# A fused attention and mixture-of-experts block on one core: the transposes of the next four tiles' rows are put at the end of the attention unit

## The chip, the cores and the metric

The kernel runs on one core of a Trainium2 chip. That core has five engines that each work through their own list of instructions in order: PE (TensorE, matrix products; the profile shows its weight loads as a row of their own, PEld), DVE (VectorE), ACT (ScalarE), POOL (GpSimd) and SP (SyncE, which here only issues DMAs). They meet through semaphores. The metric is the device time of one execution in microseconds (us), lower is better.

## The reference

The block is one layer: gated attention, then a mixture of experts, each on a layer norm of x and each added to x.

```
h  = layernorm(x)                                  # x: 32 batches x 128 tokens x 128
q, k, v    = h @ Wqkv + bqkv                       # 16 heads of 8
qa, ka, va = ctx_1024 @ Wqkv_aux + bqkv_aux
o  = softmax(q k' / sqrt 8) v * (1 - sigmoid(g)) + softmax(q ka' / sqrt 8) va * sigmoid(g)
x  = x + tanh(g_xattn) * (o @ Wo + bo)
h  = layernorm(x)
s  = sigmoid(h @ gate_w.T)                         # 64 experts in 8 groups of 8
# by s + gate_bias: the best 4 groups (sum of the two best), in them the best 8 experts
w  = 2.5 * s[chosen] / sum(s[chosen])
y  = sum over the chosen e of w_e * (silu(h @ Wg_e) * (h @ Wu_e)) @ Wd_e
y += (silu(h @ Ws_gate) * (h @ Ws_up)) @ Ws_down
x  = x + tanh(g_ffn) * y
```

All of it is float32.

## The kernel before, in words

**Two kinds of work on one list.** The 32 batches are attended in 64 units, one batch and one kind of keys (own or context) each, in the loop `for u in range(NU + 5)` near the end of the kernel. The experts' work is woven into these units, since attention alone leaves engines free. For the first seven of the eight blocks of four batches, each token's row is scattered to a table in DRAM (`xslot`), in tiles of 128 rows that belong to one expert group; there are two such tables, of 14 times four tiles and 18 times four tiles. The eighth block is computed with all experts at the end.

**A unit.** In the order of the code: `queries(u-1)` transposes the negated row maxima `nm` into PSUM (`nt`, line 580) and DVE adds them to the queries (`qa`, line 582). `scores_max(u)` makes the scores (`sp`, line 554) and DVE reduces them to `nm` (line 563, two instructions). `turn` may start a job of the experts. Then, in alternation, a step of the last batch's output (`ot`, `at`, `mt`, `msb`, `yp`: lines 639 to 667) or of the next batch's projections (`tp`, `pp`, `vp`: lines 293 to 360). `values(u-2)` is `op` (line 623), `softmax(u-1)` is the second scores `st` (line 600, it reads `qa`) and the exponentials on ACT (line 610). `add_up` finishes an earlier job: `y` (line 1054) and the next transposes `ht` (line 1041). Steps of the routing (`route`, lines 700 to 900) and scatters (line 869 on POOL, with a small memset at line 868 ahead of each) are dealt out over the unit; `use_bank` is the last place for a step that needs PSUM.

**A job** is one tile: `group_hidden` multiplies it with the gate and the up weights of its expert group (`gu`, line 1026), ACT takes the tanh (line 949), DVE multiplies twice (lines 950 and 954), POOL applies the routing weights `wq` (line 958). Two jobs later `group_turn` and `group_down` follow. Once attention is over, `alone` is true.

**Beginning four tiles.** Tiles are fetched four at a time. `load_rows_of` issues the DMA of 512 rows from the table into the only buffer `xq` (SP, line 985). `begin_tiles` reads four table entries into PE registers (line 997), transposes the four tiles on PE (line 1004), lets POOL multiply the routing columns with a mask (`wg`, line 1006), DVE reduce them to `wq` (line 1013) and ACT copy the transposes out of PSUM (`xqT`, line 1015). `pair` calls it for the next four tiles when the first job of four has just been issued.

**What sets the order.** The engines' lists are written in the order of the calls (a manual schedule), so a call that moves in the code moves its instructions on PE, POOL, DVE, ACT and SP. **PSUM:** `banks` hands out three buffers of two banks in turn, to `sp` (two), `gu`, `st` (two), `ht`, the transposes of `begin_tiles` and most routing steps; each waits for the reader of the tile that was given the same buffer three requests before. `bank` hands out two single banks in turn, to `nt`, `op`, `mt`, `ot`, `vp`, `pp`, `y` and others.

Of the kernel before, what the change touches and what calls it, by code (L numbers as in the profile page):

```python
# [51 lines left out]
def gated_block_kernel(  # L52
# [44 lines left out]
    def banks(name):  # L97
        return ps_s.tile([P, 2, 512], F32, tag="s", name=name)
# [578 lines left out]
    def scatter_some(n):  # L677

        for _ in range(min(n, len(to_scatter))):
            f, *a = to_scatter.pop(0)  # L680
            f(*a)
# [279 lines left out]
    def hidden(t, n):  # L961


        m = P if n < NPAIR else F
        if n < NPAIR and n % 2 == 0 and n:
            load_weights(t, n // 2 + 5)
        gu = banks(f"gu{t}_{n}")
        for i, (wr, ws) in enumerate(((wg_sb, wsg_sb), (wu_sb, wsu_sb))):
            lhsT = wr[:, 2 * n : 2 * n + 2, :].rearrange("p e f -> p (e f)") if n < NPAIR else ws
            nc.tensor.matmul(gu[0:m, i], lhsT, xT[t], start=True, stop=True)  # L970
        gate = cws.pop((t, n)) if n < NPAIR else None
        if t < S1:
            h = rt.tile([P, TB], F32, tag="wT", name=f"hs{t}")
        else:
            h = hp.tile([P, TB], F32, tag="h", name=f"h{t}_{n}", bufs=LAG + 1)
        return silu_times(f"{t}_{n}", m, gu, gate, alone, h)
# [4 lines left out]
    def load_rows_of(c, q):  # L981
        if q >= NQ[c]:
            return
        xq = rt.tile([P, QS, NW], F32, tag="xq", name=f"xq{c}_{q}")
        k = nc.sync.dma_start(
            out=xq,
            in_=xslot[c][q * QS * P : (q + 1) * QS * P].rearrange("(a p) d -> p a d", p=P),
        ).ins
        for name in scatters[c]:
            tc.add_manual_dep(k, name, AFTER)  # L990
        rows_of[c, q] = xq

    def begin_tiles(c, q):

        xq = rows_of.pop((c, q))
        v = [
            nc.tensor.value_load(
                table[c][0:1, q * QS + a : q * QS + a + 1], min_val=0, max_val=NG - 1
            )
            for a in range(QS)  # L1000
        ]
        tp = banks(f"xq{c}_{q}t")
        for a in range(QS):
            nc.tensor.transpose(tp[:, 0, ts(a, P)], xq[:, a, 0:D], ident)
        every = rt.tile([P, QS, EG, NG], F32, tag="wg", name=f"wg{c}_{q}")
        nc.gpsimd.tensor_tensor(  # L1006
            every,
            xq[:, :, D:NW].rearrange("p a (g e) -> p a e g", e=EG),
            mine[c][:, ts(q, QS), :].unsqueeze(2).to_broadcast([P, QS, EG, NG]),
            ALU.mult,  # L1010
        )
        wq = rt.tile([P, QS, EG], F32, tag="wq", name=f"wq{c}_{q}", bufs=2)
        V.tensor_reduce(wq, every, AX.X, ALU.add)
        xt = rt.tile([P, QS * P], F32, tag="xqT", name=f"xqT{c}_{q}", bufs=2)
        nc.scalar.copy(xt, tp[:, 0])
        parts_of[c, q] = [xt, wq, v, None]

    def group_hidden(c, q, n):

        if n == 0:  # L1020
            parts_of[c, q][3] = alone
        xt, wq, v, later = parts_of[c, q]
        gu = banks(f"gu{c}_{q}_{n}")
        for i, w in enumerate((wg_sb, wu_sb)):
            w = w.rearrange("p (g e) f -> p g (e f)", g=NG)
            nc.tensor.matmul(  # L1026
                gu[:, i],
                xt[:, ts(n, P)],
                w[:, ds(v[n], 1), :].rearrange("p o f -> p (o f)"),
                start=True,  # L1030
                stop=True,
            )
        h = hp.tile([P, TB], F32, tag="h", name=f"h{c}_{q}_{n}", bufs=LAG + 1)
        gate = wq[:, n, :].unsqueeze(2).to_broadcast([P, EG, F])
        return silu_times(f"{c}_{q}_{n}", P, gu, gate, later, h)
# [118 lines left out]
    def finish(t, ysb, w):  # L1154

        yt = bank(f"yt{t}")
        for k in range(BG // w):
            for i in range(k * w, (k + 1) * w):
                nc.tensor.transpose(yt[:, ts(i, P)], ysb[:, ts(i, P)], ident)
            xs = x_sb[t][:, ts(k, w), :]  # L1160
            V.tensor_tensor(
                xs.rearrange("p t d -> p (t d)"),
                yt[:, ts(k, w * P)],
                xs.rearrange("p t d -> p (t d)"),
                ALU.add,
            )
            b0 = t * BG + k * w
            nc.sync.dma_start(out=out[b0 : b0 + w].rearrange("b t d -> t b d"), in_=xs)
# [9 lines left out]
    alone = False  # L1178
# [22 lines left out]
    def ready(job):  # L1201
        if job[0] == "all":
            return job[1] < routed
        return job[1] in started and clock - started[job[1]] >= (2 if alone else 3)

    def pair():

        nonlocal fresh
        if todo and ready(todo[0]):
            kind, *job = todo.pop(0)  # L1210
            fresh = True
            if kind == "all":
                waiting.append((job, hidden(*job)))
            else:
                waiting.append((job, group_hidden(*job)))
                c, q, n = job
                if n == 0 and q + 1 < NQ[c]:
                    begin_tiles(c, q + 1)
                    load_rows_of(c, q + 2)


    turned = []
# [25 lines left out]
    def route_some(n, free=False):  # L1248

        nonlocal routed, takes_bank  # L1250
        for _ in range(n):
            if not routing or takes_bank and not free:
                return
            free = False
            takes_bank = next(routing[0], None)
            if takes_bank is None:
                routing.pop(0)
                routed += 1

    def use_bank():  # L1260
        if ended:
            finish(*ended.pop(0))
        else:
            route_some(1, True)
# [11 lines left out]
    def more(it):  # L1276
        next(it, None)
# [27 lines left out]
    def turn(there):  # L1305

        if there:
            pair()
        round_begins()
        scatter_some(1)  # L1310
        gather_some(1)

    for u in range(NU + 5):
        if 10 <= u:
            for k in islice(clear, 1):
                tc.add_manual_dep(k.ins, reached[min(u, NU) - 1], AFTER)
        if 1 <= u <= len(weight_loads):
            for k in weight_loads[u - 1]():
                tc.add_manual_dep(k.ins, reached[u - 1], AFTER)
        if 0 <= u - 1 < NU:  # L1320
            queries(u - 1)
        if u == 0:
            first, steps = steps, prepare(1)
            more(steps)
            more(steps)
        if u < NU:
            scores_max(u)
        if u == 0:
            finish_gates()
            more(first)  # L1330
            ictx.close()
            rt = ctx.enter_context(tc.tile_pool(name="rt", bufs=1))
            hp = ctx.enter_context(tc.tile_pool(name="hp", bufs=2))
            clear_values(1)
            count_tables()
            nc.gpsimd.memset(lower, 1.0)
            nc.gpsimd.affine_select(
                out=lower,
                in_=lower,
                compare_op=ALU.is_gt,  # L1340
                fill=0.0,
                base=0,
                pattern=[[1, NG], [-1, NG]],
                channel_multiplier=0,
            )
        k = u % UA
        n = plan(u)

        turn(n > 0)
        if k % 2 == 0:  # L1350
            more(outputs)
        else:
            more(steps)
        osb = values(u - 2) if 0 <= u - 2 < NU else None
        if osb is not None:
            finished = output((u - 2) // 2, osb)
        if 0 <= u - 1 < NU:
            softmax(u - 1)
        add_up()
        copy_some()  # L1360
        if osb is not None:
            outputs = finished
        route_some(1)
        turn(n > 1)
        more(outputs)
        copy_some()
        route_some(2)
        add_up()
        turn(n > 2)
        if u:  # L1370
            more(steps)
        route_some(1)
        add_up()
        if k == 2 and u < NU - UA - 2:
            coming = prepare((u + 2) // UA + 1)
            more(coming)
        elif k == 3:
            more(coming)
            steps, coming = coming, iter(())
        use_bank()  # L1380
        turn(False)
        copy_some()
    share_banks()
    alone = True
# [65 lines left out]
```

## Time and profile before

| | |
|---|---|
| median of 12 runs | 1046.75 us (1043.0 to 1049.41) |
| the profiled execution | 1049.55 us, its span 1047.8 us |
| mean clock granted to PE | 0.962 of full speed |
| PE busy | 942.3 us, 90% |
| DVE, POOL, ACT busy | 607.3, 540.6, 494.8 us |
| first call of `begin_tiles` (transposes) | 330.1 us |
| end of attention's weave (first `h<-th,wq` on DVE) | 602.4 us |
| transposes of `begin_tiles` in between, seven calls | 340.9, 384.0, 423.8, 469.0, 509.0, 542.9, 573.1 us |

A time "at 423.8" is counted from the start of the span. Rows of the timeline give start, duration, engine, line, what is written from what, and in brackets how long the engine had been idle before and what released it. An engine idle beside a busy PE costs nothing; PE idle during attention adds to the span unless something later gives it back.

### The profile page before, as it was taken

How to read it: one execution, taken by the hardware profiler on the slowest of the kernel's cores; microseconds unless marked ns; L12 is line 12 of the kernel's file. 1: busy time of each engine (PE TensorE's matmuls, PEld its weight loads, DVE VectorE, ACT ScalarE, POOL GpSimd, SP SyncE). 2: the span in 40 equal slices, each digit the busy share in tenths (PEclk: the TensorE clock that was granted, in tenths of full speed). 3: DMA queues.
4: the chain of work that ended last, by engine and by line, in shares of the span. 5: the costliest groups of instructions: out<-in, count | busy, mean ns of one | idle time of the engine just before them, and what ended most of it. 6: DMA issues, size and time to landing. Idle time of an engine off the chain costs nothing.

```text
span 1047.8 us, 20766 instructions
## 1 busy us (share of the span) xinstructions
PE 942.3 (90%) x7704; PEld 637.2 (61%) x7704; DVE 607.3 (58%) x1248; ACT 494.8 (47%) x943; POOL 540.6 (52%) x867
## 2 busy tenths in 40 slices
PE   6999889788897989989999799998999999999876
PEld 5777566566674666656666466665666666764332
DVE  5566776657763665575666374553455555546453
ACT  2566456454554455455544344644555555542111
POOL 3435368588576265855763767511333342007770
PEclk8899999889998999999999899999999999999989
DMA  5544234101011000100110122244222222115530
GB/s 142 129 117 151 96 116 161 44 25 48 7 39 58 22 17 24 61 19 28 39 60 16 55 81 74 78 107 113 77 84 77 76 76 69 41 51 141 142 85 25
DMA packets 100008, 75.19 MB, mean 72 GB/s; under 512 B 23943, under 2 KB 92167, under 8 KB 99911
## 3 DMA queue, kind: packets, MB, share of 16 engines
q1 hardware_dynamic: 90662, 55.11, 18.6%
q0 software_dynamic: 8960, 18.36, 5.6%
q8 instruction: 65, 1.06, 0.4%
q10 hardware_dynamic: 288, 0.39, 0.1%
q14 instruction: 33, 0.26, 0.1%
HBM read 39.63 MB, written 34.21 MB: 70 GB/s over the span
## 4 chain that ended last, share of the span: by engine, by line
PE 56%; POOL 18%; DVE 13%; issue 5%; DMA 4%; ACT 3%; SPq 1%; POOLq 0%; ACTq 0%; DVEq 0%
PE gu L1026 17%; PE y L1054 9%; PE st L600 5%; POOL yg L1095 5%; POOL xslot L869 4%; PE op L623 4%; PE ht L1041 4%; PE sp L554 4%; DVE nm L563 3%; PE pp L305 2%; PE gu L970 2%; POOL bd L268 2%; PE nt L580 2%; POOL row L234 1%; DMA yg<-yslot,place 1%
## 5 line engine op out<-in xcount | busy, mean ns | idle before, releaser
L954 DVE TENSOR_TENSOR th<-gu,th 128x512 f32<-128x512 f32 x158 | 109.0, 690 | 159.2 <-ACT th L947 157.4
L947 ACT ACTIVATE th<-gu 128x512 f32<-128x512 f32 (+1 forms) x132 | 78.9, 597 | 195.8 <-PE gu L1026 107.0
L563 DVE TENSOR_REDUCE nm<-sp 128x8 f32<-128x1024 f32 x128 | 150.7, 1218 | 18.1 <-PE sp L554 17.9
L1054 PEld LDWEIGHTS y<-wd_sb,hT 128*128 128x128 f32 x1008 | 129.7, 193 | 47.3 <-issue 45.7
L610 ACT ACTIVATE pt<-st 128x1024 f32<-128x1024 f32 x128 | 124.1, 1021 | 49.8 <-PE st L600 49.8
L1026 PE MATMUL gu<-wg_sb,xqT 128*128 x252 | 134.3, 615 | 3.1 <-DVE th L954 2.5
L1054 PE MATMUL y<-wd_sb,hT 128*128 x1008 | 136.3, 279 | 0.9 <-ACT hT L1043 0.9
L1095 POOL DMA_INDIRECT yg<-yslot,place x112 | 111.5, 995 | 43.4 <-issue 30.9
L1026 PE MATMUL gu<-wu_sb,xqT 128*128 x252 | 129.7, 596 | 0.0
L869 POOL DMA_INDIRECT xslot<-row,place x112 | 114.2, 1020 | 21.9 <-issue 20.9
L268 POOL TENSOR_SCALAR bd<-qk,mask 128x256 f32<-128x256 f32 x90 | 83.2, 934 | 45.2 <-ACT qk L321 44.5
L1006 POOL TENSOR_TENSOR wg<-xq,mine 128x256 f32<-128x256 f32 x32 | 24.6, 770 | 135.5 <-DMA xq<-xslot 121.8
L623 PE MATMUL op<-pt,v 128*32 128x128 f32 x2048 | 71.6, 282 | 25.4 <-DVE qa L582 24.8
L1026 PEld LDWEIGHTS gu<-wu_sb,xqT 128*128 128x128 f32 x252 | 48.6, 193 | 61.6 <-issue 61.6
L554 PE MATMUL sp<-bd,qk 32*128 32x256 f32 x1024 | 80.8, 421 | 5.2 <-DVE qk L319 5.2
L600 PE MATMUL st<-qa,qk 32*128 32x256 f32 x1024 | 82.4, 414 | 2.4 <-DVE nm L563 2.1
L1043 ACT COPY hT<-ht 128x512 f32<-128x512 f32 x126 | 74.0, 588 | 12.3 <-PE ht L1041 1.2
L623 PEld LDWEIGHTS op<-pt,v 128*32 128x32 f32 x2048 | 53.6, 112 | 40.1 <-DVE qa L582 29.8
L1041 PE MATMUL ht<-ident,h 128*128 128x128 f32 x504 | 76.3, 274 | 0.2 <-DVE th L954 0.2
L956 DVE TENSOR_TENSOR h<-th,wq 128x512 f32<-128x512 f32 x98 | 68.7, 701 | 3.3
L958 POOL TENSOR_TENSOR h<-th,wq 128x512 f32<-128x512 f32 x28 | 29.2, 1043 | 78.4 <-DVE th L954 62.2
L1061 ACT ACTIVATE yo<-y,tgf 128x128 f32<-128x128 f32 x126 | 46.4, 368 | 40.8 <-PE y L1054 33.0
(278 smaller groups left out, 1493.2 us busy)
## 6 DMA issues: line engine op xcount, KB each, us to landing
xslot<-zero SPq DMA_DIRECT2D x16, 768.0 KB, 3.8
xq<-xslot SPq DMA_DIRECT2D x32, 384.0 KB, 3.3
yslot<-yo SPq DMA_DIRECT2D x32, 256.0 KB, 2.4
cw<-w_dram SPq DMA_DIRECT2D x32, 256.0 KB, 4.2
x<-in_x_dram SPq DMA_DIRECT2D x16, 128.0 KB, 3.0
ctx<-in_ctx_dram SPq DMA_DIRECT2D x16, 128.0 KB, 2.6
wg_sb<-in_L_ffn_We_gate_dram SPq DMA_DIRECT2D x8, 256.0 KB, 3.6
wu_sb<-in_L_ffn_We_up_dram SPq DMA_DIRECT2D x8, 256.0 KB, 4.2
```

Source lines behind the costliest of these rows:

```text
L268: nc.gpsimd.tensor_scalar(bd[:, r, j, :], qk[:, r], mask[:, j : j + 1], None, ALU.mult)
L554: mm = nc.tensor.matmul(sp[g // 2][:, g % 2, 2 * r : 2 * r + 2, :], q[p0 : p0 + SLOT, r, ts(i, S)], kbd[p0 : p0 + SLOT, r, :, ts(i, S)], s ...
L563: V.tensor_reduce(nm[:, :, 2 * gp : 2 * gp + 2, MX].rearrange("p b g -> p g b"), sp[gp], AX.X, ALU.max, negate=True,)
L600: nc.tensor.matmul(st[g // 2][:, g % 2, 2 * r : 2 * r + 2, :], k[p0 : p0 + SLOT, r, ts(i, S)], qa[p0 : p0 + SLOT, r], start=True, stop=True,)
L610: nc.scalar.activation(pt, st[gp], AF.Exp, scale=1.0 / math.sqrt(DH))
L623: nc.tensor.matmul(op[g * SLOT : (g + 1) * SLOT, r], v[:, i, g, 2 * r + j, :], pt[g // 2][:, g % 2, 2 * r + j, :], start=j == 0, stop=j == 1,)
L869: k = nc.gpsimd.indirect_dma_start(out=xslot[c], out_offset=IndirectOffsetOnAxis(ap=place[c][:, i0 + i, r : r + 1], axis=0), in_=row[:, i, :],
L954: V.tensor_tensor(th[0:m], gu[0:m, 1], th[0:m], ALU.mult)
L1026: nc.tensor.matmul(gu[:, i], xt[:, ts(n, P)], w[:, ds(v[n], 1), :].rearrange("p o f -> p (o f)"), start=True, stop=True,)
L1041: nc.tensor.transpose(ht[:, 0, ts(p, P)], h[:, ts(p, P)], ident)
L1054: nc.tensor.matmul(y[:, 0:D], hs[:, ts(p, P)], w[:, ds(v[n], 1), p, :].rearrange("p o d -> p (o d)"), start=p == 0, stop=p == GP - 1,)
L1095: nc.gpsimd.indirect_dma_start(out=k["yg"][:, n, r, :], out_offset=None, in_=yslot[c], in_offset=IndirectOffsetOnAxis(ap=place[c][:, 2 * k ...
```

## The change

The call for the next four tiles is no longer made where the first job of four is issued. `pair` notes it in `to_begin`, and the unit makes it at its end, behind `use_bank`. Once attention is over (`alone`) it is made at once, as before. Nothing is added or taken away: only seven calls move, those of the first table's tiles 1 to 7 (in groups of four). On each engine's list the instructions of such a call stand later:

```diff
+    to_begin = []
+
+    def begin_next():
+
+        if to_begin:
+            c, q = to_begin.pop()
+            begin_tiles(c, q)
+            load_rows_of(c, q + 1)
+
     def pair():
...
                 if n == 0 and q + 1 < NQ[c]:
-                    begin_tiles(c, q + 1)
-                    load_rows_of(c, q + 2)
+                    to_begin.append((c, q + 1))
+                    if alone:
+                        begin_next()
...
         use_bank()
+        begin_next()
         turn(False)
         copy_some()
```

On PE the register reads and the four transposes move from behind the first `gu` of the unit to just ahead of the next unit's `nt`. On ACT the copy moves behind the unit's `hT` copy. On DVE `wq` moves to just ahead of the next unit's `qa` in calls 1 to 6. On POOL `wg` moves behind the unit's scatters, `xn` and routing steps. On SP the order of the DMAs is the same. In the buffers of two banks the transposes no longer take the place between `gu` and `st`.

## The prediction

> **What bounds the kernel now.** I read the page first: engines, slices, costliest groups.
>
> ```profile
> PE 942.3 (90%) x7704; PEld 637.2 (61%) x7704; DVE 607.3 (58%) x1248; ACT 494.8 (47%) x943; POOL 540.6 (52%) x867
> PEclk8899999889998999999999899999999999999989
> L1006 POOL TENSOR_TENSOR wg<-xq,mine 128x256 f32<-128x256 f32 x32 | 24.6, 770 | 135.5 <-DMA xq<-xslot 121.8
> ```
>
> PE is the bound; what moves is small work beside it. So the question is only where PE stands still in the seven units concerned, before and after. That is in the timeline, read around the transposes (line 1004). Call 3, with the unit behind it:
>
> ```profile
> 423.83 0.63 PE L1004 MATMUL xq_3t<-ident,xq 128*128 128x128 f32 x4 [0.51 <-DVE nm L563]
> ...
> 429.30 0.75 POOL L1006 TENSOR_TENSOR wg<-xq,mine 128x256 f32<-128x256 f32 x1
> 430.08 0.42 DVE L1013 TENSOR_REDUCE wq<-wg 128x32 f32<-128x256 f32 x1 [4.62 <-POOL between L868]
> 431.14 0.68 DVE L582 TENSOR_TENSOR qa<-nt,bd 128x512 f32<-128x512 f32 x1
> 434.05 1.08 PE L623 MATMUL op<-pt,v 128*32 128x128 f32 x32
> 435.06 1.15 PE L600 MATMUL st<-qa,qk 32*128 32x256 f32 x16
> 436.13 1.16 PE L1054 MATMUL y<-wd_sb,hT 128*128 x8
> 436.23 0.87 POOL L717 TENSOR_SCALAR sc<-sc 128x256 f32<-128x256 f32 x1
> ```
>
> DVE waits 4.62 us in front of `wq` for POOL. Here that harms nobody: `qa` still comes 3.9 us ahead of `st`. POOL is late by itself: its L717 runs 6 us after the `lg` it belongs to (429.24 to 430.24). The unit at 371 shows what a late `qa` costs:
>
> ```profile
> 372.72 0.68 DVE L582 TENSOR_TENSOR qa<-nt,bd 128x512 f32<-128x512 f32 x1
> 373.46 1.08 PE L623 MATMUL op<-pt,v 128*32 128x128 f32 x32 [1.75 <-DVE qa L582]
> 375.72 1.13 PE L600 MATMUL st<-qa,qk 32*128 32x256 f32 x12 [0.43 <-DVE nm L563]
> 376.78 1.16 PE L1054 MATMUL y<-wd_sb,hT 128*128 x8
> ```
>
> `op` takes the single bank that `nt` had and waits until `qa` has read it; `st` then waits for the two `nm` behind `qa` on DVE. So the next matmul group (`y`) starts 376.78 - 372.72 = 4.06 us after `qa` starts. That interval is my ruler.
>
> **The change, call by call.** *What goes away:* PE's idle time in front of the transposes: 0.71, 0.70, 0.51, 1.52, 0.09, 0.37, 0.92 us in calls 1 to 7, 4.8 us in all. In calls 2 and 4 the transposes start as the first `nm` ends (383.9, 468.9): they wait for the buffer of `sp`. In the others nothing ends just then; I take it for the four register reads (line 997), which move along, so at their new place they may cost 0.1 to 0.9 us again.
>
> *What is added:* `wq` now stands directly ahead of `qa` on DVE, and DVE works in order. `wq` needs `wg`, and `wg` stands on POOL behind the unit's other work. Wherever POOL gets there late, `qa`, `nm`, `st` and PE are late. I follow POOL's list with the durations of before.
>
> *Call 2.* POOL runs `bd` to 387.7, `h` to 388.7, `x` 0.73, `xn` 1.58 (to 391.0), the five small ones from `nxt` on (1.44 from 391.69 to 393.13; now to 392.5), `wg` 0.76 (393.3). `wq` 0.42: `qa` starts at 393.65 (before 390.70), `y` at 397.7 by the ruler. Before it started at 396.11: +1.6.
>
> *Call 3.* POOL: `h` ends at 429.34. Then a scatter with memset 1.31 (430.65), `x` 0.74 (431.4), two scatters at 1.26 (433.9), `xn` 1.58 (435.5), L717 0.87 (436.4), `wg` 0.75 (437.1), `wq` 0.42. `qa` starts at 437.55 instead of 431.14, `y` at 441.6 instead of 436.13: +5.5. PE is idle from the end of `mt` (some 433.5) to 438.3: 4.8 us.
>
> *Call 4.* Here `wg` stands behind the routing chain. DVE: `sel` ends at 474.4 (`ot` is 0.8 earlier). POOL: L783 0.73 (475.2), `xn` 1.58 (476.8), L791 0.61, L792 0.86 (478.3), `pf` 0.19 and 0.77 (479.3), `wg` 0.75 (480.05). `wq` to 480.5, `qa` at 480.45 instead of 477.55, `y` at 484.5 instead of 481.58: +2.9; PE idle about 3.4 us in one piece.
>
> *Call 5.* POOL: `h_4_1` follows L954, which ends at 517.3 without the transposes ahead of it: 518.4. Two scatters at 1.28 (521.0), `wg` 0.75, `wq` 0.42: `qa` at 522.15 instead of 518.64, `y` at 526.2 instead of 523.95: +2.3.
>
> *Calls 1 and 6.* POOL is through early (346.4 and 549.8, where DVE reaches `wq` at 349.8 and 550.35). `st` no longer waits for the transposes, but in call 1 PE runs into the wait for `hs` (1.61 us at 348.60) all the same. Gains of 0.3 and 0.4 against a new register-read bubble: 0, between -0.7 and +0.6 each.
>
> *Call 7.* Not `qa` but the next job's L950 follows. Before, DVE's L667 waited behind `wq` (576.23); now the chain L667, L837, POOL's L840 to L887 starts about 1.6 us earlier, pays `wg` and `wq` (1.2) later, and part of that overlaps DVE's own work: 1.1 us earlier at L950. PE waits on the end of this chain (the 5.98 us ahead of L706 at 587.77): -1.1, between -1.2 and +0.5.
>
> *Covered at nothing:* ACT's copy (0.59 each; ACT is idle beside it, and `xqT` is not read for four jobs). The DMA of the next rows leaves SP some 3 to 7 us later, lands in 3.3 us and is needed 30 us later; behind it on SP stand only context loads and `yslot` stores, which wait for later work anyway. The buffers now go to `sp`, `gu`, `st` in a shifted turn, each free by then.
>
> *The clock.* Long PE idling costs more than itself:
>
> ```profile
> 318.00:322.00 4.00, 0.50 (x2) 0.14 (x1) 0.17 (x1) 2.28 (x5) 3.56 (x7) 1.00 0.15 51
> 322.00:326.00 4.00, 2.79 (x16) 1.90 (x19) 0.61 (x1) 1.39 (x3) 3.78 (x6) 0.61 0.05 18
> 326.00:330.00 4.00, 1.37 (x16) 0.58 (x8) 2.44 (x3) 0.00 (x0) 2.94 (x4) 0.50 0.46 137
> 350.00:354.00 4.00, 4.00 (x22) 2.25 (x21) 2.81 (x5) 0.00 (x0) 0.00 (x0) 0.57 0.02 4
> 370.00:374.00 4.00, 2.25 (x27) 1.35 (x30) 3.79 (x13) 0.75 (x2) 1.94 (x2) 1.00 0.00 0
> ```
>
> Columns: stretch, length, busy PE, PEld, DVE, ACT, POOL, granted clock, DMA share, GB/s. After 3.50 us of idling (318.18 to 321.68) the clock is 0.61 and 0.50; after 1.61 us (ahead of 348.60) 0.57 for one stretch; 1.75 us at 371.71 leave it at 1.00. A stretch at 0.57 costs 4.0 x 0.43 = 1.7 us; 0.61 and 0.50 cost 4.0 x (0.39 + 0.50) = 3.6. Call 3 idles 4.8 us, nearest to the 3.50 row, which had a second idle piece in it: I take 2.6, between 1.7 and 3.6. Call 4, 3.4 us and busier around, lies between 371 (0) and 318 (3.6): 1.3. Calls 2 and 5 idle under 2 us in a piece: 0, at most 1.7.
>
> The Trainium skill (TensorE: Matmul & The Clock Gate, Part 1) has the clock halve after at least one idle window of about 3.4 us, the window running free. The 0.57 after only 1.61 us does not fit it. By the rule alone only call 3 would surely pay, one window at half, an estimate of 1.7 us, and the whole would come to some 2 us less than mine.
>
> *Sum:* calls 1 to 7: 0 + 1.6 + 5.5 + 2.9 + 2.3 + 0 - 1.1 = 11.2; clock 3.9; together +15.1 us on the profiled 1049.55. That execution lies 2.8 above the median of 1046.75. I take 1061 us for the median after (+14; a little given back where later chains find POOL less behind).
>
> **The rivals.**
> *A, faster:* POOL reaches `wg` before DVE is through with the unit, so `qa` is not held. Then only the idle time ahead of the transposes counts: 1046.75 - 4.8 = 1042. For it: calls 1 and 6 are like that. Against: in call 3 POOL would have to be there 6.4 us sooner than its list allows. It decides where calls 2 to 5, which lose 12.3 here with the freed idle time already in it, lose less than the 1.1 of call 7.
> *B, little left:* PE's delay gives POOL time, and the later stalls of PE on POOL and DVE (0.85 at 457.6, 0.58 at 499.1, 1.67 at 537.8) vanish, with no clock loss: 11.2 - 3.1 = 8: 1055. Against: each of them is a chain that starts from its own unit's PE work.
> *C, the clock falls in calls 2 to 5:* 11.2 + 3.6 + 3.6 + 1.7 + 1.7 = 22: 1069. For it: 0.57 after 1.61 us. Against: 1.00 after 1.75.
>
> **How the numbers follow.** My case 0.55, B 0.22, C 0.13, A 0.10. The low end lies between B and A, at 1049; the high end short of C's full price, at 1068: about 1 in 10 is left out on each side. What differs by 0.2% (2.1 us) can be told from no change. Of A, 0.07 is faster and 0.02 the same, the rest a small loss; B leaves 0.02 for the same: faster 0.07, same 0.04, slower 0.89.
>
> **What would show it.** In the changed profile: `wq` directly ahead of `qa`, after a DVE wait released by POOL; `op` (line 623) behind calls 2 to 5 with idle time released by `qa`, longest behind call 3 (near 4.8 us); PEclk lower in the slice at 440; no wait on `nm` ahead of the transposes. The prediction is wrong if `op`'s idle time there stays under 1 us, or if the time is lost after attention (past 605).

## The result and the profile after

The changed kernel takes 1066.49 us in the median of 8 runs (1065.86 to 1071.88), the kernel before in the same comparison 1046.94 us (34 runs): a ratio of 1.0201, 95% interval 1.0185 to 1.0218, so slower by 19.5 us. Its profiled execution took 1065.97 us, with a span of 1064.3 us and a mean granted clock of 0.954 (before 1049.55, 1047.8 and 0.962).

First the page of the changed kernel: engines, PE's clock by slices, and two of the costly groups.

```profile
PE 954.2 (90%) x7704; PEld 647.1 (61%) x7704; DVE 609.0 (57%) x1248; ACT 495.4 (47%) x943; POOL 541.0 (51%) x867
PEclk9999999899997899898999899999999999999989
L1006 POOL TENSOR_TENSOR wg<-xq,mine 128x256 f32<-128x256 f32 x32 | 24.7, 771 | 132.8 <-DMA xq<-xslot 132.7
L623 PE MATMUL op<-pt,v 128*32 128x128 f32 x2048 | 72.9, 286 | 30.3 <-DVE qa L582 29.8
```

The line for `op` in the page of the kernel before:

```profile
L623 PE MATMUL op<-pt,v 128*32 128x128 f32 x2048 | 71.6, 282 | 25.4 <-DVE qa L582 24.8
```

DVE, ACT and POOL do the same work in the same time. PE is busy 11.9 us longer with the same 7704 instructions: that is not more work but a slower clock (the seven slices from 319 us on read 7, 8, 9, 9, 8, 9, 8, where the line of before reads 8, 9, 9, 9, 9, 9, 9). And `op` now waits 29.8 us for `qa`, 5.0 more than the 24.8 of before. Call 3 in the timeline of the changed kernel:

```profile
431.87 0.63 PE L1004 MATMUL xq_3t<-ident,xq 128*128 128x128 f32 x4 [1.18 <-ACT sc L716]
...
437.13 0.87 POOL L717 TENSOR_SCALAR sc<-sc 128x256 f32<-128x256 f32 x1
437.97 0.74 POOL L1006 TENSOR_TENSOR wg<-xq,mine 128x256 f32<-128x256 f32 x1
438.74 0.42 DVE L1013 TENSOR_REDUCE wq<-wg 128x32 f32<-128x256 f32 x1 [8.04 <-POOL between L868]
439.08 0.68 DVE L582 TENSOR_TENSOR qa<-nt,bd 128x512 f32<-128x512 f32 x1
439.81 1.08 PE L623 MATMUL op<-pt,v 128*32 128x128 f32 x32 [3.44 <-DVE qa L582]
442.08 2.08 PE L600 MATMUL st<-qa,qk 32*128 32x256 f32 x12 [0.27 <-DVE nm L563]
444.08 2.08 PE L1054 MATMUL y<-wd_sb,hT 128*128 x8
```

This is the chain that the prediction drew: DVE stands 8.04 us in front of `wq`; POOL's L717, then `wg`, then `wq`, then `qa`, and PE stands until `op` may start. Behind it `st` and `y` take 2.08 us each, where before `st` took 1.15 and `y` 1.16. The windows of the changed kernel (stretch, length, busy PE, PEld, DVE, ACT, POOL, granted clock, DMA share, GB/s) say why:

```profile
348.00:352.00 4.00, 4.00 (x25) 2.87 (x26) 0.84 (x2) 0.59 (x1) 0.00 (x0) 0.50 0.36 102
...
440.00:444.00 4.00, 3.68 (x48) 2.12 (x40) 3.30 (x4) 0.99 (x2) 0.51 (x1) 0.67 0.35 115
444.00:448.00 4.00, 4.00 (x16) 2.96 (x15) 0.00 (x0) 2.27 (x4) 3.41 (x7) 0.50 0.14 49
```

The kernel before at its call 3 (there `y` starts at 436.13):

```profile
436.00:440.00 4.00, 4.00 (x24) 2.31 (x21) 0.00 (x0) 2.99 (x5) 3.54 (x7) 1.00 0.07 25
440.00:444.00 4.00, 2.59 (x25) 2.08 (x26) 3.59 (x8) 0.86 (x2) 3.35 (x7) 1.00 0.21 72
```

Behind call 3 of the changed kernel PE is busy for 7.68 of the 8 us, most of them at half speed. The same happens behind call 2 (0.77 and 0.80 from 388 to 396), call 4 (0.57 and 0.58 from 492 to 500) and ahead of call 6 (0.68 and 0.90 from 556 to 564). Values such as 0.77 are means over a switch: in windows laid on its edges the clock is 0.50 for 3.41 us behind call 2 (390.17 to 393.58) and for 6.82 us behind calls 3 and 4 (441.37 to 448.19, 492.57 to 499.39), and 1.00 in the 3.4 us before and after each. Behind the first transposes something else is new, in the timeline around call 1:

```profile
345.00 1.33 PE L728 MATMUL sh<-wsd_sb,hs 64*128 64x128 f32 x8 [1.62 <-DVE hs L952]
347.86 1.08 PE L1004 MATMUL xq_1t<-ident,xq 128*128 128x128 f32 x4 [1.52 <-issue]
```

The idle time ahead of the transposes has not gone: it is 1.52, 1.46, 1.18, 1.26, 0.86, 0.87 and 1.90 us in calls 1 to 7, 9.1 in all, against 4.8 before.

**Where the time went.** I compare the start of a unit's `nt` in both traces; a growing distance is a loss in that stretch. From the unit ahead of call 1 to the transposes of the last routing step (L706, 661.25 before, 678.48 after) the stretch grows from 324.63 to 344.11 us: +19.5. PE's idle time in it grows from 30.3 to 38.9 us (+8.6). The clock's price, each 4 us slice's busy PE time multiplied by one minus its granted clock, grows from 5.3 to 14.7 us (+9.4). These two make 18.0 of the 19.5. Nothing more is lost once attention is over. That this trace's 19.5 equals the difference of the medians is chance in part: the two profiled executions differ by 16.4 us as a whole, since the changed one is 2.3 us ahead where the stretch begins.

| call | 1 | 2 | 3 | 4 | 5 | 6 | 7 | sum |
|---|---|---|---|---|---|---|---|---|
| forecast, clock included | 0 | +1.6 | +8.1 | +4.2 | +2.3 | 0 | -1.1 | +15.1 |
| measured in the trace | +1.5 | +2.3 | +8.3 | +5.4 | +2.2 | +2.2 | -2.5 | +19.4 |

### The profile page after: what moved, and what is told of

Read it like the earlier page. It is cut to its first block, busy times and chain, and to the rows that moved or that the text cites. A ratio compares the mean times of both kernels' runs of the same rounds, so it can differ in the third digit from the quotient of the medians.

```text
span 1064.3 us, 20769 instructions
## 1 busy us (share of the span) xinstructions
PE 954.2 (90%) x7704; PEld 647.1 (61%) x7704; DVE 609.0 (57%) x1248; ACT 495.4 (47%) x943; POOL 541.0 (51%) x867
## 4 chain that ended last, share of the span: by engine, by line
PE 51%; POOL 21%; DVE 12%; issue 6%; DMA 4%; ACT 3%; SPq 1%; POOLq 0%; ACTq 0%; DVEq 0%
PE gu L1026 15%; PE y L1054 8%; POOL xslot L869 6%; POOL yg L1095 5%; PE st L600 5%; PE ht L1041 4%; PE op L623 4%; PE sp L554 3%; DVE nm L563 3%; POOL bd L268 2%; PE pp L305 2%; PE gu L970 2%; POOL row L234 1%; PE nt L580 1%; DMA xq<-xslot 1%
## 5 line engine op out<-in xcount | busy, mean ns | idle before, releaser
L563 DVE TENSOR_REDUCE nm<-sp 128x8 f32<-128x1024 f32 x128 | 150.6, 1218 | 16.4 <-PE sp L554 16.2
L623 PE MATMUL op<-pt,v 128*32 128x128 f32 x2048 | 72.9, 286 | 30.3 <-DVE qa L582 29.8
L600 PE MATMUL st<-qa,qk 32*128 32x256 f32 x1024 | 88.6, 429 | 4.6 <-DVE nm L563 4.0
L600 PEld LDWEIGHTS st<-qa,qk 32*128 32x128 f32 x1024 | 54.0, 196 | 25.4 <-DVE nm L563 11.5
```

Of the source, the lines that this page charges most:

```text
L563: V.tensor_reduce(nm[:, :, 2 * gp : 2 * gp + 2, MX].rearrange("p b g -> p g b"), sp[gp], AX.X, ALU.max, negate=True,)
L600: nc.tensor.matmul(st[g // 2][:, g % 2, 2 * r : 2 * r + 2, :], k[p0 : p0 + SLOT, r, ts(i, S)], qa[p0 : p0 + SLOT, r], start=True, stop=True,)
L623: nc.tensor.matmul(op[g * SLOT : (g + 1) * SLOT, r], v[:, i, g, 2 * r + j, :], pt[g // 2][:, g % 2, 2 * r + j, :], start=j == 0, stop=j == 1,)
```

## The experiments

The first seven ran on two chips on which the kernel before takes 1077.27 (the first four) and 1074.61 us (the next three), so ratios are what is compared; the changed kernel itself was not run on these two. The last two ran on a chip where it takes 1046.69. There is one profile of the kernel before, that of the comparison above, and every trace here is set against it.

**1. `wq` out of the way of `qa`.** The changed kernel, but DVE's reduction to `wq` is put behind the next unit's `qa`, `nm` and first job; everything else stays moved.

```diff
-        V.tensor_reduce(wq, every, AX.X, ALU.add)
+        if alone:
+            V.tensor_reduce(wq, every, AX.X, ALU.add)
+        else:
+            to_reduce.append((wq, every))
...
         turn(n > 0)
+        reduce_late()
```

> The changed kernel, but only the reduce to wq on DVE is put off once more, behind the next unit's qa, nm and first job (transposes, register reads, copy and POOL's wg stay at the end of the unit). Theory (qa is held by wq, which waits for POOL): the idle time of PE ahead of op behind calls 3 and 4 (3.44 and 2.14 us) goes to under 0.5, the clock behind it stays at 1.00, and of the loss of 19.5 us some 13 to 16 come back: 1051 us (1048 to 1055). Rival (it is the place of PE's own transposes, their register reads and the turn of the PSUM buffers): the time stays at 1062 to 1067.

1082.6 us, ratio 1.0054 (1.0031 to 1.0077). Call 3 in its timeline:

```profile
442.72 0.63 PE L1005 MATMUL xq_3t<-ident,xq 128*128 128x128 f32 x4 [1.51 <-ACT sc L716]
...
443.82 0.69 DVE L582 TENSOR_TENSOR qa<-nt,bd 128x512 f32<-128x512 f32 x1 [2.60 <-PE nt L580]
...
447.15 1.08 PE L623 MATMUL op<-pt,v 128*32 128x128 f32 x32
...
448.42 0.75 POOL L1007 TENSOR_TENSOR wg<-xq,mine 128x256 f32<-128x256 f32 x1
449.20 0.42 DVE L1215 TENSOR_REDUCE wq<-wg 128x32 f32<-128x256 f32 x1 [0.29 <-POOL between L868]
```

`wg` is as late as ever, but nobody waits: `op` starts without idle time, and the units around calls 3 and 4 lose nothing (from the unit of call 3 to the one behind call 4 the distance to the kernel before goes from 13.1 to 12.9 us). About three quarters of the loss go with this one instruction's place (2.01% becomes 0.54%, on another chip). What is left stands ahead of the transposes: 1.78, 1.47, 1.51 us and so on. Call 2 keeps its whole step: +2.3 us here, +2.3 in the changed kernel.

**2. The opposite: only `wg`, `wq` and the next load moved.** The kernel before, with register reads, transposes and copy at the old place; `weigh` holds the lines that make `wg` and `wq`.

```diff
+        if alone or q == 0:
+            weigh(c, q, xq)
+        else:
+            to_weigh.append((c, q, xq))
...
         use_bank()
+        if to_weigh:
+            c, q, xq = to_weigh.pop()
+            weigh(c, q, xq)
+            load_rows_of(c, q + 1)
```

> The kernel before, but of the seven calls in attention only POOL's wg, DVE's wq and the next load go to the end of the unit; register reads, transposes and copy stay where they were. Theory: most of the loss is there, since qa again waits for wq behind calls 2 to 5: 1060 us (1056 to 1065), with op idle for over 2 us behind call 3. Rival (place of the transposes): no loss, 1045 to 1049.

1102.79 us, ratio 1.0227 (1.0165 to 1.0288): the whole loss, with not one transpose moved, and more than the 1060 us (a ratio of 1.013) that I had expected. In its trace the units of calls 3 and 4 lose 15.1 us (13.0 in the changed kernel) and those around call 6 another 6.4 (2.2). Its timeline at call 3:

```profile
444.89 0.74 POOL L1018 TENSOR_TENSOR wg<-xq,mine 128x256 f32<-128x256 f32 x1
445.67 0.42 DVE L1025 TENSOR_REDUCE wq<-wg 128x32 f32<-128x256 f32 x1 [6.78 <-POOL between L868]
446.00 0.68 DVE L582 TENSOR_TENSOR qa<-nt,bd 128x512 f32<-128x512 f32 x1
446.74 1.93 PE L623 MATMUL op<-pt,v 128*32 128x128 f32 x32 [3.99 <-DVE qa L582]
```

The title of the change names the transposes, but their move is not what costs. `op` behind them takes 1.93 us here instead of 1.08: the clock again.

**3. The register reads left at the old place.** The changed kernel, with line 997's four reads behind the first `gu`.

```diff
                     to_begin.append((c, q + 1))
+                    if not alone:
+                        read_of[c, q + 1] = read_groups(c, q + 1)
```

> The changed kernel, but the four register reads stay behind the first gu, as before; the transposes are at the end of the unit. Theory (the idle time of 0.86 to 1.90 us ahead of the transposes at their new place is the register reads, which PE's list now meets with little work queued ahead of them): that idle time goes to under 0.3 us, 0.1 to 0.9 us of it turn up behind gu, and since calls 2 to 5 are set by qa only calls 1, 6, 7 and the clock gain: 1063 us (1060 to 1066). Rival (they wait for the PSUM buffer or for ACT's copy): the idle time stays, 1066 us.

1099.01 us, ratio 1.0207 (1.0169 to 1.0245). The idle time ahead of the transposes is gone (under 0.3 us), so it was the register reads; but no time is won, and I had expected some 3 us. At call 3:

```profile
433.18 0.61 PE L1010 MATMUL xq_3t<-ident,xq 128*128 128x128 f32 x4
...
439.96 0.74 POOL L1012 TENSOR_TENSOR wg<-xq,mine 128x256 f32<-128x256 f32 x1
440.74 0.42 DVE L1019 TENSOR_REDUCE wq<-wg 128x32 f32<-128x256 f32 x1 [7.38 <-POOL between L868]
441.07 0.68 DVE L582 TENSOR_TENSOR qa<-nt,bd 128x512 f32<-128x512 f32 x1
441.81 1.93 PE L623 MATMUL op<-pt,v 128*32 128x128 f32 x32 [4.15 <-DVE qa L582]
```

PE comes earlier and waits longer: 4.15 us at `op` instead of 3.44. While `qa` decides, what stands ahead of it on PE is free. That holds for calls 3 to 5. In call 1 the trace is 3 us better than the changed kernel's, and around call 6 as much worse: there `st` waits 1.62 us for `nm`, and the clock is at half behind it. In call 2, where the changed kernel's `op` has no idle time, `op` now waits 0.85 us for `qa`, and the step is +1.5 instead of +2.3.

**4. PE kept busy while it waits.** The changed kernel with useless products into a free part of `mt`'s bank, 10 in call 3's unit and 6 in call 4's.

```diff
+        for n in range(busy.pop() if busy else 0):
+            nc.tensor.matmul(mt[:, ts(3, S)], ident, ident, start=True, stop=True)
...
+            if c == 0 and q in FILL:
+                busy.append(FILL[q])
+
+    FILL = {3: 10, 4: 6}
```

> The changed kernel with useless matrix products (128x128 of ident by ident, 10 behind call 3, 6 behind call 4) put between mt and op, where PE stands still for 3.44 and 2.14 us; what they write is not read. Theory (the stall costs more than itself, since the granted clock falls to 0.50 behind it): the clock stays at 1.00 at 440 to 448 and 494 to 498 and 3 to 6 us come back although PE does more: 1062 us (1060 to 1064). Rival (the clock is not on the path, DVE and POOL set the pace there anyway): 1066 to 1068.

1093.04 us, ratio 1.0137 (1.0098 to 1.0176). Timeline and windows behind call 3:

```profile
445.76 2.40 PE L662 MATMUL mt<-ident 128*128 128x128 f32 x20
...
448.25 0.68 DVE L582 TENSOR_TENSOR qa<-nt,bd 128x512 f32<-128x512 f32 x1
...
448.99 1.08 PE L623 MATMUL op<-pt,v 128*32 128x128 f32 x32 [0.83 <-DVE qa L582]
```

```profile
448.00:452.00 4.00, 2.69 (x48) 1.81 (x48) 3.97 (x6) 0.64 (x2) 1.10 (x1) 1.00 0.43 123
452.00:456.00 4.00, 4.00 (x22) 2.13 (x19) 0.51 (x1) 2.81 (x5) 2.96 (x5) 1.00 0.07 25
```

By the medians the loss falls from 2.0 to 1.4%, although PE does more work; but these are 4 runs, and their interval overlaps that of the changed kernel in experiment 9 (1.0158 to 1.0208). The trace shows where it comes from. `qa` is as late, but the clock behind it is 1.00. The unit of call 3 now loses 4.4 us (7.6 in the changed kernel from the same unit to the next), that of call 4 2.8 (5.4): so some 3.3 and 2.5 us of these two losses were the clock, not the wait. They are 5.8 of the 6.4 us by which the stretch from the unit ahead of call 1 to the last L706 is shorter than the changed kernel's.

**5. Both costs taken away.** Experiments 1 and 3 together: `wq` late, register reads early, all else moved.

> The change with both its costs taken away: the wq reductions put off behind the next unit's qa and nm, and the four register reads left at their old place behind the first gu group. My theory (loss = qa held by wq, plus the register-read bubbles that stay once qa is free): the bubbles of 0.9 to 1.8 us ahead of the transposes vanish as in the run with the reads early, and no wait on qa takes their place. The run with wq late alone lost 0.5% (5 us); the seven bubbles there are 9.6 us, of which I expect about half in the end (other waits move up): ratio 0.998 to 1.002. Rival (the rest of the loss, 0.5%, is not the bubbles but the later start of wg, wq and xqT themselves, or the shifted buffers): ratio stays at 1.004 or more.

1072.76 us, ratio 1.0002 (0.9979 to 1.0025). Timeline and one window at call 3:

```profile
434.28 0.61 PE L1011 MATMUL xq_3t<-ident,xq 128*128 128x128 f32 x4
...
435.37 0.69 DVE L582 TENSOR_TENSOR qa<-nt,bd 128x512 f32<-128x512 f32 x1 [0.90 <-PE nt L580]
...
438.69 1.08 PE L623 MATMUL op<-pt,v 128*32 128x128 f32 x32
...
441.45 0.42 DVE L1221 TENSOR_REDUCE wq<-wg 128x32 f32<-128x256 f32 x1 [0.99 <-POOL between L868]
```

```profile
436.00:440.00 4.00, 4.00 (x52) 2.39 (x49) 3.34 (x5) 0.86 (x3) 3.64 (x6) 1.00 0.14 49
```

The whole loss is gone, though the transposes, `wg`, the copy and the next load of all seven calls are still at the unit's end. So the rest that experiment 1 left was the reads' idle time with what it does to the clock: there the windows showed 0.53 and 0.62 behind call 1 and 0.57 behind call 2; here no window of 4 us from 340 to 588 is under 0.95. In the stretch from the unit ahead of call 1 to the last L706 it is even 3.1 us shorter than before in the trace (1.2 of this in the unit behind call 1, where the clock stays at 1.00 behind the wait on `hs`, and 1.4 in call 4, whose idle time of 1.52 us is gone), but the interval of the times does not let this be called a gain.

**6. Only calls 1, 6 and 7 moved.**

```diff
-                    if alone:
+                    if alone or q + 1 not in (1, 6, 7):
                         begin_next()
```

> Only calls 1, 6 and 7 are put off; calls 2 to 5 stand at the old place. My theory, that each call's loss comes from its own unit: the steps of the changed kernel at these calls, +1.5, +2.2 and -2.5 us, remain, +1.2 in all: ratio 1.000 to 1.003, no op wait on qa above 0.5 us behind calls 3 and 4, clock there as before. Rival (the late calls lose because every call before them is late, POOL's backlog being carried from unit to unit): calls 6 and 7 behave differently when calls 2 to 5 are on time, and the ratio is off this by more than 0.3%.

1075.18 us, ratio 1.0014 (0.9994 to 1.0033), as my theory had it; calls 2 to 5 carry the loss. In its timeline `op` behind call 3 starts without idle time, and call 1 pays for its reads, right behind the wait on `hs`:

```profile
350.91 1.13 PE L728 MATMUL sh<-wsd_sb,hs 64*128 64x128 f32 x8 [1.61 <-DVE hs L952]
353.81 0.63 PE L1004 MATMUL xq_1t<-ident,xq 128*128 128x128 f32 x4 [1.77 <-issue]
```

In the trace call 1 costs 0.9 us and call 7 gains 1.5, against +1.5 and -2.5 in the changed kernel's. Call 6 costs only 0.6 us here, not 2.2. The next run says why.

**7. Only call 7 moved.** As experiment 6, with `(7,)` for the list.

> Only call 7 is put off; all others at the old place. By the prediction's step for call 7 (chain L667, L837, POOL's L840 to L887 earlier): -1.1 us; by the changed kernel's trace -2.5 us: ratio 0.9975 to 0.9990, faster by 0.1 to 0.25%, and the stall ahead of L706 shrinks from about 6 us to 3.5 to 5. Rival (the -2.5 was only slack won by the earlier lateness of PE, POOL having had time to catch up): ratio 1.000 and the stall as before.

1072.0 us, ratio 0.9985 (0.9963 to 1.0007): what I expected in size, but not to be told from no change. The stall ahead of L706 is 3.56 us instead of 5.98, as in the changed kernel, so call 7's gain is its own. Call 6 stands at its old place here, and yet the clock falls ahead of it. Timeline and windows of this run:

```profile
542.24 1.13 PE L728 MATMUL sh<-wsd_sb,hs 64*128 64x128 f32 x8 [1.67 <-DVE hs L952]
```

```profile
540.00:544.00 4.00, 2.33 (x16) 1.74 (x16) 3.24 (x6) 0.59 (x1) 2.51 (x5) 0.95 0.22 75
544.00:548.00 4.00, 4.00 (x21) 2.17 (x21) 2.68 (x4) 0.00 (x0) 0.00 (x0) 0.62 0.00 0
```

The same wait of the same work in the kernel before, timeline and windows:

```profile
537.78 1.13 PE L728 MATMUL sh<-wsd_sb,hs 64*128 64x128 f32 x8 [1.68 <-DVE hs L952]
```

```profile
536.00:540.00 4.00, 2.32 (x25) 1.94 (x28) 3.69 (x7) 0.20 (x1) 2.02 (x3) 1.00 0.21 74
540.00:544.00 4.00, 3.63 (x30) 1.90 (x26) 3.50 (x5) 1.08 (x3) 0.00 (x0) 1.00 0.00 0
```

The same 1.7 us idle leaves the clock at 1.00 in one execution and costs 1.5 us in another. In the changed kernel it is 0.68 and 0.90 at this place. So most of what its trace books on call 6 is this, and not the call.

**8. The register reads spread.** The kernel before, call 7 alone moved, and of tiles 2 to 7 (in groups of four) three of the four reads taken one at a time behind earlier jobs' `gu`.

```diff
                 c, q, n = job
+                if not alone and n and q + 2 < NQ[c]:
+                    read_of.setdefault((c, q + 2), []).append(read_group(c, q + 2, n - 1))
```

> The kernel before, with call 7 alone put off and, for tiles 2 to 7, three of the four register reads taken one at a time behind the gu groups of earlier jobs; the fourth stays ahead of the transposes. My theory (four reads in a row outlast the PE work queued ahead of them; one or two do not): the idle time ahead of the transposes falls in calls 3, 5, 6 (0.51, 0.09, 0.37 us before) to under 0.2 us and in call 7 (1.90 us when put off) to under 1 us; calls 2 and 4 keep 0.70 and 1.52, since there sp's buffer is waited for. With call 7's chain started earlier: ratio 0.996 to 0.9985. Rival (a read costs PE its time wherever it stands): the idle time moves behind the other gu groups, ratio 0.999 or more.

1046.36 us, ratio 0.9994 (0.9978 to 1.0009). The mechanism holds, the gain does not come. The timeline of call 7 and of the next routing step:

```profile
573.22 0.60 PE L1008 MATMUL xq_7t<-ident,xq 128*128 128x128 f32 x4
...
580.78 0.63 PE L1045 MATMUL ht<-ident,h 128*128 128x128 f32 x4 [1.28 <-DVE th L954]
...
585.53 0.48 PE L706 MATMUL xtp<-ident,row 128*128 128x128 f32 x1 [4.13 <-POOL row L234]
```

A single read ahead of the transposes costs no idle time (1.90 us with four at this place). But PE then comes earlier to the wait on POOL's rows, 4.13 us instead of 3.56, with a new 1.28 ahead of it: the trace is 2.8 us ahead at the next routing step (658.47 against 661.25), and the median of 12 runs is not. Of these 2.8 us, 1.6 arise behind call 1, where the clock stays at 1.00 this time; so it does in experiment 7, which changes nothing there.

**9. The changed kernel again**, beside the same runs as experiment 8.

> The changed kernel itself, beside the same runs of the kernel before as the others here. All theories: ratio 1.017 to 1.023; the trace's stalls behind calls 3 and 4 on qa again 2 to 3.5 us and a granted clock near 0.5 behind them. If the clock behind these stalls were 1.00 here, the clock's share of the loss would depend on when the gate looks.

1066.27 us, ratio 1.0183 (1.0158 to 1.0208). `op` waits 3.37 and 2.15 us behind calls 3 and 4, and the windows behind call 3 are again

```profile
440.00:444.00 4.00, 3.39 (x48) 2.30 (x48) 3.73 (x5) 0.57 (x2) 0.49 (x2) 0.73 0.39 123
444.00:448.00 4.00, 4.00 (x17) 2.82 (x14) 0.00 (x0) 2.58 (x4) 3.40 (x7) 0.50 0.07 26
```

None of the versions beats the kernel before by what can be measured.

## Why the prediction was right, and where its sizes were off

**The sign and the mechanism were right.** `wq` stands directly ahead of `qa`, waits there for POOL, and `op` and `st` are late behind it. Experiment 1 takes this away and three quarters of the loss with it, experiment 2 makes it alone and has all of it. Counted from the `nt` of the unit in which the call is made, `qa` starts within 0.2 us of the forecast in calls 2 to 5 (call 3: 17.76 us against 17.82). The time, 1066.49, lies inside the range but 5.5 us above the likeliest, and nearer to rival C's 1069.

**Calls 3 and 5 came as worked out** from POOL's list of before: +8.3 and +2.2 against 8.1 and 2.3. In call 5 the ruler holds to the digit: `qa` starts at 537.38, `y` at 541.44, 4.06 us later. PE's wait was given as 4.8 us in call 3 and 3.4 in call 4; `op` waited 3.44 and 2.14, because the reads' idle time of 1.18 and 1.26 us ahead of the transposes already holds PE back. With the reads early (experiment 3) the waits are 4.15 and 3.58. Less the clock's price by windows (given below) the steps of calls 3 and 4 are 5.1 and 2.1, against 5.5 and 2.9.

**Call 2 came near for another reason.** Forecast was +1.6 from a late `qa`, measured +2.3. But in the changed kernel `op` behind call 2 starts without idle time, and experiment 1, which takes `wq` out of the way, leaves the +2.3 as it is. There it is the reads' idle time (1.46 us instead of 0.70) and the clock behind it. The forecast cause is real but covered: it shows once the reads are early (experiment 3: +1.5). So the listed sign "`op` behind calls 2 to 5 with idle time released by `qa`" is seen plainly in calls 3 and 4 alone; in call 5 it is 0.12 us at `op` and 0.43 at `st`.

**The term that failed is the clock.** It was set at 2.6 for call 3, 1.3 for call 4, and nothing for the others: 3.9. It measures 9.4 over the stretch. By windows the changed kernel pays 2.7 in call 1 (the kernel before 1.6 there), 1.4 in call 2 (1.7 in the window on its edges), 3.2 in call 3, 3.3 in call 4 and 1.7 ahead of call 6. The step "calls 2 and 5 idle under 2 us in a piece: 0" was wrong for call 2. For call 4 I chose 1.3, between 0 and 3.6, and the upper bound was right: it idles in two pieces, 1.26 and 2.14 us, not in one of 3.4, and loses the clock all the same. Rival C, which has the clock fall in calls 2 to 5 (1069), described the clock better than my case, save for call 5 and with call 1 missing.

**The register reads were under-priced.** I let them cost "0.1 to 0.9 us again" at the new place. They cost 0.86 to 1.90 at the unit's end. That it is the reads, experiments 3, 5 and 8 show: they remove the idle time by moving them. Why they cost more here than behind `gu` (less PE work ahead of them is my guess) is not shown. The reading that "nothing ends just then" in call 3 of before was wrong (the second `nm` ends at 423.80, the transposes start at 423.83), but it did no harm: in experiment 8 the transposes of call 3 start at 421.86, before that `nm` ends (422.50). In calls 3 to 5 this is hidden, since `qa` decides there (experiment 3). In call 1 it is not, and it falls right behind the wait on `hs`: "0, between -0.7 and +0.6" became +1.5. Call 6's "0" was no worse than 0.6 by experiment 6; the rest of its +2.2 is clock that also falls without the change (experiment 7).

**Call 7 was right in kind and small in size:** -2.5 in the trace, forecast -1.1. The chain to L706 is 1.4 us earlier against the unit before it, in experiment 7 too; the other 1.0 is clock behind the shorter stall (0.50 for two stretches before, for one after).

**The rivals.** A (POOL reaches `wg` in time) is excluded by `op`'s waits of 3.44 and 2.14 us. B (later stalls vanish) did not happen: those it names are 0.84 us (at 467.5), 0.58 (at 514.4) and 1.68 (at 555.3) after, 0.85, 0.58 and 1.68 before. "A little given back" from 15 to 14 is not seen either.

**The rule weighed in the prediction.** By the Trainium skill (TensorE: Matmul & The Clock Gate, Part 1) the clock halves after at least one idle window of about 3.4 us. Here no idle piece in calls 1, 2 and 4 is longer than 2.14 us, and the clock fell to 0.50, 0.77 and 0.57: as a threshold the rule would have left these losses out. The same section has the window running free: it does not reset when the kernel starts. This trace has such a grid: in the changed kernel the half-clock stretches from call 1 to call 6 start at 345.8, 390.2, 441.4, 492.6 and 557.4, which are 13, 15, 15 and 19 times 3.41 us apart. But neither the length of the idle time nor its place on the grid tells here what happens. In the changed kernel 1.75 us ahead of `op` at 372.71 leave the clock at 1.00, and 1.46 us ahead of 389.54 halve it. The two pieces of experiment 7 each lie inside one stretch of their grid (534.5 to 537.9, 540.2 to 543.6), and only one halves the clock. Why stays open; for pieces of 1.3 to 2 us a price for the clock is an average at best.

## What to carry to other kernels

When a step moves, look at what then stands behind each of its instructions on its own engine: here a 0.42 us reduction, which no one needed for four jobs, was put ahead of the one instruction that PE waits for, behind the list of an engine that is late by itself. A late consumer should stand late and its producer early; with the reduction behind `qa` the loss fell from 2.0 to 0.5%. And where PE is the bound, price its stalls of some 1.5 us and more with the clock that may fall behind them: here that doubled them (8.6 us more idle time, 9.4 of clock).

## What the hardware showed that I had not expected

- Half the loss is the granted clock: 0.50 for 3.4 or 6.8 us behind idle pieces of 1.3 to 3.4 us. With useless products of 2.40 us in call 3's wait it stayed at 1.00 there (experiment 4; ratio 1.0137 against 1.0201).
- The same idle piece (1.7 us ahead of L728) cost nothing in one execution and had the clock at 0.62 in another.
- Four register reads in a row on PE cost 0.86 to 1.90 us at the unit's end, and in call 7 none when three of the four are spread behind matmuls (experiment 8).
